# A four-layer graph network on one core: gathered rows as three bf16, and a layer's last blocks in one piece

## The chip, the core and the metric

The kernel runs on one core of a Trainium2 chip. The core has a matrix engine (TensorE, in the profile PE for matmuls and PEld for weight loads), VectorE (DVE), ScalarE (ACT) and GpSimd (POOL); SyncE (SP) issues most of the DMAs, and POOL issues the indirect ones, the gathers. The engines run on their own, each working through its own queue in order, and wait for each other by semaphores. The metric is the time of one execution on the device in microseconds.

## The reference

```python
N, E, C, NOUT, NL = 6250, 100000, 256, 64, 4

def agg(h):
    return jax.ops.segment_sum(h[src], dst, num_segments=N)

h = relu(layernorm(x0))          # 6250 x 256
x = h
for l in range(NL - 1):
    h = x + agg(x)
    h = relu(h @ W1s[l] + b1s[l])
    h = relu(h @ W2s[l] + b2s[l])
    x = h @ W3s[l] + b3s[l]
h = x + agg(x)
h = relu(h @ cW1 + cb1)
h = relu(h @ cW2 + cb2)          # 6250 x 64
out = x0 + (h @ cW3 + cb3)
```

All data are fp32. `src` and `dst` are drawn at random, and the edges come sorted by `dst`. So each of four layers sums, for every node, the rows of the nodes that point to it (16 on average), adds the node's own row, and sends the result through three matrices. In the kernel these are layers 0 to 3.

## The kernel before

The 6250 nodes are 49 blocks of 128 (the last has 106). `any_edges` is a fallback for inputs that are not as expected and does not run here; `sorted_edges` does the work. The next layer's first matrix is applied ahead: W3 of a layer is multiplied with W1 of the next once, early, so that each layer's table in DRAM (`tables[l]`, fp32, 256 columns) holds rows that have been through W1 already, and aggregation is done on those.

A layer aggregates its destination blocks in two ways, side by side.

- **Panels.** For 29 of the 49 blocks (25 in layer 0) the adjacency is kept as dense counts (uint8, built in layer 0, stored in DRAM as `mat`). A panel is 3 or 4 destination blocks. `product` runs over the 49 source blocks j of a panel, one *tick* each: four matmuls (L1334) of `XY[:, j]`, the rows of block j as an upper and a lower float32r part, against `a`, the counts cast from uint8 by ACT or DVE (`prepare`, three ticks ahead, AHEAD), into two PSUM tiles `agg`.
- **Gathered blocks.** The other 20 blocks (24 in layer 0) are done from lists of edges. Each block's edges stand in two halves of nine tiles of 128 edges. POOL issues one indirect DMA for each tile (L1198), which fetches 128 rows of the table into `rows`; DVE makes one-hot matrices `hot` (L1223); PE multiplies them (L1242) into `sums`. Each matmul has 32 stationary columns and uses one of four column strips of PE, chosen by half and quarter. A block is done in two *visits*, of three rounds each. In the trace a matmul of fp32 appears as two records.

Then `finish` adds the node's own row (`own`), transposes the result (L1264) and after the last block of a run calls `mlp`; `product` calls it for its panel. `mlp` spreads its work over the coming ticks: `second` (L1099, W2, with a relu on ACT), `third` (L1122, W3 times next W1, with the bias added on DVE into `z`, L1131) and `store`, which writes `z` to the next layer's table and, when all parts of the layer are kept, begins the next layer (`layers[l + 1].begin`).

**What sets the order.** The program order is written out by hand: each engine's queue is filled in the order of the calls. `tick` advances a clock `now` and runs what is `due`; `later(n, f)` puts f off by n ticks. A plan of the cost of each tick (`when`) spreads the visits of a layer evenly from LEAD = 75 units after `begin` to TAIL = 8 ticks before the layer's last tick. Gathers are issued up to three visits ahead. A gather of layer l + 1 reads rows from everywhere, so the first waits for the last store of layer l. As the last panel of a layer frees block j of `XY` (`used`), the next layer's rows are loaded back from the table (`back`, BACK = 3 at a time) or taken from `z` directly, and split into the upper part (ACT, L1055) and the lower (DVE, L1056).

**At a layer's end** the last gathered run is block 48 alone (`gone[-1]`), and the last panel is blocks 44 to 47 (40 to 43 in layer 0). Both go through `mlp` with `hurry`, their steps laid between the first ticks of the next layer's first panel.

Buffers that the change touches: `rows` 24 in layer 0 and 26 after it, `a` AHEAD + 4 after layer 0, `xt` 3 and `z` 2 in the last layer, `zz` 3.

Of the kernel before, what the change touches and what calls it, by code (L numbers as in the profile page):

```python
# [17 lines left out]
P = 128  # L18
# [378 lines left out]
def sorted_edges(  # L397
# [92 lines left out]
    eps = const.tile([P, 1], F32, name="eps")  # L490
    tables = [dram.tile([N, C], F32, name=f"table{l}") for l in range(NLAYER + 1)]
    w31d = [dram.tile([P, (KC + 1) * C], F32, name=f"w31_{l}") for l in range(NLAYER)]
    mats = [dram.tile([P, n, NT * P], U8, name=f"mat{p}") for p, (_, n) in enumerate(panels)]
# [407 lines left out]
    with tc.manual_schedule():  # L901
# [36 lines left out]
        def load_weights(l):  # L938
            w2 = load_w("w2", W2s[l] if l < NLAYER else cW2, work, nc.sync)
            if l < NLAYER:  # L940
                w3 = work.tile([P, KC + 1, C], F32, name="w3")
                nc.sync.dma_start(out=w3.rearrange("p k c -> p (k c)"), in_=w31d[l])
            else:
                w3 = late.tile([NOUT, C], F32, name="cw3", bufs=1)
                nc.sync.dma_start(out=w3, in_=cW3)
                row = late.tile([P, C], F32, name="cb3r", bufs=1)
                nc.sync.dma_start(out=row, in_=bass.AP(tensor=cb3.tensor, offset=cb3.offset,
                                                       ap=[[0, P], [1, C]]))
                w3 = (w3, row)
            weights[l] = w2, w3  # L950
# [88 lines left out]
        def later(n, fn):  # L1039
            due.append((now[0] + n, fn))  # L1040

        def tick():
            now[0] += 1
            run = [f for t, f in due if t <= now[0]]
            due[:] = [(t, f) for t, f in due if t > now[0]]
            for f in run:
                f()


# [3 lines left out]
        def split(j, m, z):  # L1053

            nc.scalar.copy(XY[:, j:j + m, :C], z[:, :m, :])  # L1055
            later(1, lambda: nc.vector.tensor_tensor(XY[:, j:j + m, C:], z[:, :m, :],  # L1056
                                                     XY[:, j:j + m, :C].bitcast(F32), OP.subtract))

        def reload(l, j):

            if (l, j) in used and (l, j) in kept and l < NLAYER:
                wanted.append((l, j))
                bring()
# [16 lines left out]
        def given():  # L1080
            lent[0] -= 1
            bring()

        def mlp(l, b0, n, h1, hurry):

# [18 lines left out]
            def third(i):  # L1104
                m = min(2, n - i)
                w3 = weights[l][1]
                if end:
                    xt = late.tile([P, 2, C], F32, name="xt", bufs=3)
                    if b0 + i + m == NT and LAST < P:
                        nc.vector.memset(xt[:, m - 1, :], 0.0)  # L1110
                    rows_io(x, b0 + i, m, xt, True)
                    nc.vector.tensor_tensor(xt[:, :m, :], xt[:, :m, :],
                                            w3[1][:, None, :].to_broadcast([P, m, C]), OP.add)
# [11 lines left out]
                if end:  # L1125
                    z = late.tile([P, 2, C], F32, name="z", bufs=2)
                    later(2, lambda: nc.vector.tensor_tensor(z[:, :m, :], v, xt[:, :m, :], OP.add))  # L1127
                    later(4, lambda: rows_io(out, b0 + i, m, z, False))
                    return
                z = work.tile([P, 2, C], F32, name="zz", bufs=3)  # L1130
                later(2, lambda: nc.vector.tensor_tensor(  # L1131
                    z[:, :m, :], v, w3[:, KC:, :].to_broadcast([P, m, C]), OP.add))

                def store():
                    rows_io(tables[l + 1], b0 + i, m, z, False)
                    blocks = range(b0 + i, b0 + i + m)
                    kept.update((l, j) for j in blocks)
                    if all((l, j) in used for j in blocks):
                        split(b0 + i, m, z)
                    else:  # L1140
                        for j in blocks:
                            reload(l, j)
                    if sum(1 for k, _ in kept if k == l) == NT:
                        layers[l + 1].begin(now[0])
                        later(1, lambda: load_weights(l + 1))

                later(3 - hurry, store)

# [9 lines left out]
        class Gathered:  # L1158
# [24 lines left out]
            def send(self, upto):  # L1183
                while self.sent < min(upto, self.n):
# [8 lines left out]
                    for k in self.tiles(rounds):  # L1193
                        for h in range(2):
                            t = gath.tile([P, C], F32, name="rows")
                            self.rows[g, h, k] = t
                            o = self.blocks[g][3] + h * TS + k
                            nc.gpsimd.indirect_dma_start(  # L1198
                                out=t, out_offset=None, in_=tables[self.l][:, :],
                                in_offset=bass.IndirectOffsetOnAxis(ap=idx[:, o:o + 1], axis=0),  # L1200
                            )
# [12 lines left out]
            def one_hots(self, v):  # L1214
# [3 lines left out]
                for r in rounds:  # L1218
                    hot = work.tile([P, 2, 2, Q], F32, name="hot", bufs=6)
                    for i, k in enumerate(ROUNDS[r]):  # L1220
# [8 lines left out]
            def add(self):  # L1229
# [8 lines left out]
                for r in rounds:  # L1238
                    for h in range(2):
                        for m, k in enumerate(ROUNDS[r]):  # L1240
                            if k is not None:
                                nc.tensor.matmul(  # L1242
                                    self.sums[(2 * h + m) * Q:(2 * h + m + 1) * Q, :C],
                                    self.hots[r, m][:, h, :], self.rows[g, h, k], start=(r == 0),
                                    stop=(r == (len(ROUNDS) - 2 if m == 0 else len(ROUNDS) - 1)))
                self.done += 1
# [5 lines left out]
            def finish(self, b, n, g, sums, own):  # L1252
                u = work.tile([P, C], F32, name="u", bufs=1)
                later(1, lambda: nc.vector.tensor_tensor(u, sums[:, :C], own[:, 0, :], OP.add))  # L1254
                if g == 0:
# [3 lines left out]
                def turn():  # L1259
# [11 lines left out]
                    if g == n - 1:  # L1271
                        mlp(self.l, b, n, h1, b == gone[-1][0])

# [9 lines left out]
        ahead = [2, 3]  # L1283
        LEAD, TAIL = 75, 8

# [30 lines left out]
        def product(l, p, ps_a, beside):  # L1316
# [25 lines left out]
            for c in range(KC):  # L1342
# [3 lines left out]
                else:  # L1346
                    nc.scalar.activation(h1[:, c, :w], agg[c][:, :w], AF.Relu,  # L1347
                                         bias=b1[l][:, c:c + 1])
            mlp(l, b0, n, h1, hurry)

# [13 lines left out]
        with tc.tile_pool(name="hots", bufs=1) as hots, tc.tile_pool(  # L1364
            name="ats", bufs=1
        ) as ats, tc.tile_pool(name="rings", bufs=AHEAD + 2) as rings, tc.tile_pool(
            name="gath", bufs=24
        ) as gath, tc.tile_pool(
# [17 lines left out]
        late = ctx.enter_context(tc.tile_pool(name="late", bufs=1))  # L1386
        rings = ctx.enter_context(tc.tile_pool(name="rings2", bufs=AHEAD + 4))
        gath = ctx.enter_context(tc.tile_pool(name="gath2", bufs=26))
        ps_a = ctx.enter_context(tc.tile_pool(name="ps_a2", bufs=4, space=PSUM))
# [68 lines left out]
```

## Time and profile before

| what | value |
|---|---|
| time, median of three runs | 2240.57 us (2235.93 to 2242.09) |
| the profiled execution's own time | 2230.63 us |
| its span, first to last instruction | 2228.8 us |
| granted TensorE clock, mean | 0.983 |
| gathers, L1198 | 1512, 982 ns each, 1484.3 us of POOL |
| panel matmuls, L1334 | 6076, 1454.7 us of PE |
| sums matmuls, L1242 | 3696 records, 281.5 us of PE |
| second and third matmuls, L1099 and L1122 | 164.3 and 140.0 us of PE |
| DMA | 395.56 MB, mean 177 GB/s |

A row of the table of groups gives the instruction's line, the engine, what it writes and reads, its count, then its busy time and its mean duration. Matmuls are pipelined, so the records overlap and a group's busy time is not the number of records times the mean. Where the text below speaks of the time of a group of matmuls, it is from the start of its first to the start of what follows on PE. The stages are: preparation and normalisation (0 to 188 us), layer 0 with the building of the counts (to 733), layers 1 (to 1231), 2 (to 1728) and 3 (to 2215), and the end. By windows, as busy us of the engine:

| window | PE | DVE | ACT | POOL | DMA share |
|---|---|---|---|---|---|
| 188 to 733 | 533.71 | 300.13 | 350.52 | 402.93 | 0.61 |
| 733 to 1231 | 490.72 | 164.42 | 160.52 | 347.89 | 0.58 |
| 1231 to 1728 | 491.31 | 162.47 | 159.26 | 349.09 | 0.57 |
| 1728 to 2215 | 471.75 | 166.80 | 142.56 | 350.60 | 0.59 |

### The profile page before, as it was taken

What the parts mean: (1) busy time and instruction counts of PE and PEld (TensorE: products, weight loads), DVE (VectorE), ACT (ScalarE), POOL (GpSimd) and SP (SyncE); (2) the same over time, 40 slices, a digit from 0 to 9 for tenths busy, and PEclk for the clock granted to TensorE, in tenths of its full rate; (3) what the DMA queues carried; (4) which work ended last, traced back from release to release, by engine and by line L of the source; (5) the groups of instructions that cost most, each with busy time, mean ns of one, the idle gap of its engine ahead of it and who ended that gap; (6) DMA issues with size and microseconds to landing.
All of it is one profiled execution on the core that took longest, in us unless ns stands there. A gap on an engine that the chain in (4) does not pass through costs nothing.

```text
span 2228.8 us, 35398 instructions
## 1 busy us (share of the span) xinstructions
PE 2118.0 (95%) x12356; PEld 1559.5 (70%) x12356; DVE 918.2 (41%) x2723; ACT 920.1 (41%) x1915; POOL 1521.5 (68%) x1570
## 2 busy tenths in 40 slices
PE   4778999999999999999999999999999999999998
PEld 2555766667776777778877777778877766677765
DVE  6667465445656522223323422223323423333332
ACT  3666565666667422223334322322324423222222
POOL 2337777777776477777774577777774577777773
PEclk9888999999999999999999999999999999999999
DMA  5436575565666655555655655555655655666663
GB/s 173 134 120 201 185 227 173 178 211 174 200 205 225 195 168 172 165 156 170 193 167 172 191 173 169 157 161 180 187 163 166 204 173 177 184 184 186 191 186 102
DMA packets 264100, 395.56 MB, mean 177 GB/s; under 512 B 36353, under 2 KB 210028, under 8 KB 263912
## 3 DMA queue, kind: packets, MB, share of 16 engines
q0 software_dynamic: 73920, 200.88, 30.2%
q1 hardware_dynamic: 187936, 189.68, 26.8%
q10 hardware_dynamic: 2056, 2.65, 0.4%
q8 instruction: 99, 1.62, 0.3%
q14 instruction: 89, 0.73, 0.1%
HBM read 335.81 MB, written 57.26 MB: 176 GB/s over the span
## 4 chain that ended last, share of the span: by engine, by line
PE 65%; DMA 4%; issue 2%; POOL 1%; ACT 0%; DVE 0%; SPq 0%; POOLq 0%; DVEq 0%
PE agg L1334 45%; PE sums L1242 8%; PE ps L1099 5%; PE ps L1122 4%; DMA rows<-table,idx 3%; POOL rows L1198 1%; PE ps L1119 1%; PE pt L1264 1%; PE bp L1010 1%; DMA xt<-in_x_dram 0%; ACT h L1347 0%; DMA own<-table 0%; DVE z L1127 0%; ACT at L1017 0%; ACT h L1268 0%
## 5 line engine op out<-in xcount | busy, mean ns | idle before, releaser
L1198 POOL DMA_INDIRECT rows<-table,idx x1512 | 1484.3, 982 | 614.0 <-issue 243.5
L1334 PE MATMUL agg<-a,XY 128*128 128x512 f32 (+1 forms) x6076 | 1454.7, 386 | 3.6 <-ACT a L1310 3.2
L1334 PEld LDWEIGHTS agg<-a,XY 128*128 128x128 f32 x6076 | 1085.4, 189 | 239.1 <-issue 81.0
L1310 ACT CAST a<-at 128x512 fp32r<-128x512 uint8 (+1 forms) x943 | 537.0, 579 | 650.3 <-PE agg L1334 585.2
L1312 DVE CAST a<-at 128x512 fp32r<-128x512 uint8 (+1 forms) x576 | 279.6, 490 | 498.7 <-PE agg L1334 455.0
L1242 PE MATMUL sums<-rows,hot 128*32 128x256 f32 x3696 | 281.5, 387 | 31.9 <-DMA rows<-table,idx 30.4
L1242 PEld LDWEIGHTS sums<-rows,hot 128*32 128x32 f32 x3696 | 119.4, 110 | 169.7 <-issue 54.7
L1017 ACT CAST at<-bp 128x392 uint8<-128x392 f32 x348 | 161.1, 490 | 142.8 <-PE bp L1010 139.9
L1099 PE MATMUL ps<-h,w 128*128 128x512 f32 (+5 forms) x392 | 164.3, 541 | 1.2 <-ACT h L1347 1.2
L1254 DVE TENSOR_TENSOR u<-sums,own 128x256 f32<-128x256 f32 x84 | 35.5, 423 | 291.7 <-PE sums L1242 291.7
L1010 PE MATMUL bp<-hi,lo 128*128 128x196 bf16 x928 | 136.0, 259 | 19.9 <-DVE hi L969 11.7
L1223 DVE TENSOR_TENSOR hot<-colf,rel 128x64 f32<-128x64 f32 x924 | 140.6, 217 | 12.3 <-PE sums L1242 11.9
L1122 PE MATMUL ps<-w,h 128*128 128x256 f32 x588 | 140.0, 379 | 0.0
L1010 PEld LDWEIGHTS <-lo 128*128 128x128 bf16 x928 | 71.9, 100 | 94.8 <-issue 43.9
L969 DVE TENSOR_TENSOR lo<-lanes,pairs 128x512 bf16<-128x512 bf16 x232 | 97.1, 419 | 84.0 <-PE bp L1010 58.4
L969 DVE TENSOR_TENSOR hi<-cols,pairs 128x784 bf16<-128x784 bf16 x232 | 129.6, 559 | 0.0
L1122 PEld LDWEIGHTS ps<-w,h 128*128 128x128 f32 x588 | 111.0, 189 | 15.7
L1268 ACT ACTIVATE h<-pt,bias 128x256 f32<-128x256 f32 (+1 forms) x92 | 36.9, 453 | 199.1 <-PE pt L1264 199.1
L1101 ACT ACTIVATE h<-ps,bias 128x512 f32<-128x512 f32 (+5 forms) x98 | 62.4, 637 | 109.6 <-PE ps L1099 109.6
L1131 DVE TENSOR_TENSOR zz<-ps,w 128x512 f32<-128x512 f32 (+1 forms) x81 | 51.7, 638 | 130.9 <-PE ps L1122 130.9
L1099 PEld LDWEIGHTS ps<-h,w 128*128 128x128 f32 (+1 forms) x392 | 68.2, 181 | 51.3 <-issue 29.4
L1019 DVE CAST at<-bp 128x392 uint8<-128x392 f32 x116 | 65.5, 565 | 91.9 <-PE bp L1010 90.3
(134 smaller groups left out, 716.6 us busy)
## 6 DMA issues: line engine op xcount, KB each, us to landing
at<-mat SPq DMA_DIRECT2D x133, 448.0 KB
at<-mat SPq DMA_DIRECT2D x84, 336.0 KB
rows<-table,idx POOLq DMA_INDIRECT x1512
mat<-at SPq DMA_DIRECT2D x29, 784.0 KB
table<-zz SPq DMA_DIRECT2D x66, 256.0 KB
back<-table SPq DMA_DIRECT2D x126, 128.0 KB
own<-table SPq DMA_DIRECT2D x80, 128.0 KB
xs<-in_x_dram SPq DMA_DIRECT2D x8, 768.0 KB
```

The lines of the kernel that those rows point to most:

```text
L969: nc.vector.tensor_tensor(o.rearrange("p q (n t) -> p q n t", t=2), values.rearrange("p (n t) -> p n t", t=2)[:, None, :, :].to_broadcast( ...
L1010: nc.tensor.matmul(bp[:, m * HW:(m + 1) * HW], lo[:, q + m, :], hi[:, q + m, :], start=True, stop=True)
L1017: nc.scalar.copy(o, v)
L1019: nc.vector.tensor_copy(o, v)
L1099: nc.tensor.matmul(ps[:mp, :w], weights[l][0][:, c, i * P:i * P + mp], h1[:, c, :w], start=(c == 0), stop=(c == KC - 1))
L1122: nc.tensor.matmul(o, h2[0][:, c, nodes], w3[:, c, :], start=(c == 0), stop=(c == KC - 1))
L1198: nc.gpsimd.indirect_dma_start(out=t, out_offset=None, in_=tables[self.l][:, :], in_offset=bass.IndirectOffsetOnAxis(ap=idx[:, o:o + 1], a ...
L1223: nc.vector.tensor_tensor(hot[:, i, :, :], colf[:, None, i * Q:(i + 1) * Q].to_broadcast([P, 2, Q]), rel[:, o + k:o + k + TS + 1:TS, None] ...
L1242: nc.tensor.matmul(self.sums[(2 * h + m) * Q:(2 * h + m + 1) * Q, :C], self.hots[r, m][:, h, :], self.rows[g, h, k], start=(r == 0), stop= ...
L1310: nc.scalar.copy(o, mat[l, p][j])
L1312: nc.vector.tensor_copy(o, mat[l, p][j])
L1334: nc.tensor.matmul(agg[c][:, :w], XY[:, j, o:o + P], a[:, :w], start=(j == 0 and half == 0), stop=(j == NT - 1 and half == 1))
```

## The change

Three things, in layers 1 to 3 and at the ends of layers 0 to 2.

1. Beside each table there is now `thirds[l - 1]`, the same rows as three bf16 parts whose sum is the fp32 value: 768 bf16, 1536 bytes a row in place of 1024. `store` puts each finished block on a list `waiting`; `in_thirds` makes the parts in four steps (ACT copies, DVE subtracts, ACT copies, DVE subtracts) and stores them; `one_step`, called once each tick, moves all jobs one step and starts a new one every three ticks. `tri` has two buffers, `left` one. Gathers of layers 1 to 3 read `thirds`, the one-hots are bf16, and each tile and strip has two bf16 matmuls: 512 columns (parts one and two side by side) and 256 columns (part three onto part one). `finish` adds both halves of `sums`.
2. The last run and the last panel of layers 0 to 2 no longer go through `mlp`. When both are there, `close` runs at one tick: four `second` steps, three `third` steps, the stores, then the thirds of all blocks that are left (`finish_thirds`), and only then `begin` of the next layer. Relus alternate between ACT and DVE.
3. TAIL goes from 8 to 5. Buffers: `rows` 22 and 23, `a` AHEAD + 3, `xt` 2; the last layer's `z` shares `zz`; the last layer's weights share the buffer of `w3`.

```diff
+    thirds = [dram.tile([N, 3 * C], BF16, name=f"thirds{l}") for l in range(1, NLAYER + 1)]
@@ tick
             for f in run:
                 f()
+            one_step()
@@
+        thirding, waiting = [], []
+
+        def in_thirds(l, j, z, of):
+            tri = work.tile([P, 1, 3 * C], BF16, name="tri", bufs=2)
+            t = [tri[:, 0, i * C:(i + 1) * C] for i in range(3)]
+            nc.scalar.copy(t[0], z)
+            yield
+            left = work.tile([P, C], F32, name="left", bufs=1)
+            nc.vector.tensor_tensor(left, z, t[0], OP.subtract)
+            yield
+            nc.scalar.copy(t[1], left)
+            yield
+            nc.vector.tensor_tensor(t[2], left, t[1], OP.subtract)
+            rows_io(thirds[l - 1], j, 1, tri, False)
+
+        def one_step():
+            for a in list(thirding):
+                a[1] += 1
+                if next(a[0], True):
+                    thirding.remove(a)
+            if waiting and (not thirding or thirding[-1][1] > 2):
+                a = waiting.pop(0)
+                job = in_thirds(*a)
+                next(job)
+                thirding.append([job, 1, a[3]])
+
+        def finish_thirds(upto):
+            while any(a[-1] <= upto for a in thirding + waiting):
+                one_step()
...
+        def rows_tile():
+            made[0] += 1
+            finish_thirds(made[0] - 3)
+            return work.tile([P, 2, C], F32, name="zz", bufs=3)
@@
+        def store(l, b, m, z, of):
+
+            blocks = range(b, b + m)
+            waiting.extend((l + 1, j, z[:, j - b, :], of) for j in blocks)
+            rows_io(tables[l + 1], b, m, z, False)
...
+        def close(l, run, panel):
...
+            def second(key, i):
...
+                ps = ps_m.tile([P, W], F32, name="ps")
+                for c in range(KC):
+                    nc.tensor.matmul(ps[:, :w], w2[:, c, i * P:(i + 1) * P], h1[:, c, :w],
+                                     start=(c == 0), stop=(c == KC - 1))
+                if i == 0:
+                    nc.scalar.activation(h2[b0][:, i, :w], ps[:, :w], AF.Relu,
+                                         bias=b2[l][:, i:i + 1])
+                else:
+                    nc.vector.tensor_scalar(h2[b0][:, i, :w], ps[:, :w], b2[l][:, i:i + 1], 0.0,
+                                            op0=OP.add, op1=OP.max)
...
+            for key in (run, panel):
+                for i in range(KC):
+                    second(key, i)
+            for key in (run, panel):
+                for i in range(0, key[1], 2):
+                    third(key, i)
+            finish_thirds(made[0])
+            free[0] = now[0] + 2
+            assert sum(1 for k, _ in kept if k == l) == NT
+            layers[l + 1].begin(now[0])
+            later(1, lambda: load_weights(l + 1))
@@ send
-                            t = gath.tile([P, C], F32, name="rows")
+                            if self.l:
+                                t = gath.tile([P, 3 * C], BF16, name="rows")
+                            else:
+                                t = gath.tile([P, C], F32, name="rows")
...
-                                out=t, out_offset=None, in_=tables[self.l][:, :],
+                                out=t, out_offset=None,
+                                in_=thirds[self.l - 1][:, :] if self.l else tables[0][:, :],
@@ add
+                            if self.l:
+
+                                nc.tensor.matmul(o, self.hots[r, m][:, h, :], t[:, :2 * C],
+                                                 start=(r == 0), stop=False)
+                                nc.tensor.matmul(o[:, :C], self.hots[r, m][:, h, :], t[:, 2 * C:],
+                                                 start=False, stop=stop)
@@ finish
+                def gather_up():
+                    nc.vector.tensor_tensor(u, sums[:, :C], own[:, 0, :], OP.add)
+                    if self.l:
+                        nc.vector.tensor_tensor(u, sums[:, C:], u, OP.add)
@@
-        LEAD, TAIL = 75, 8
+        LEAD, TAIL = 75, 5
@@
-        rings = ctx.enter_context(tc.tile_pool(name="rings2", bufs=AHEAD + 4))
-        gath = ctx.enter_context(tc.tile_pool(name="gath2", bufs=26))
+        rings = ctx.enter_context(tc.tile_pool(name="rings2", bufs=AHEAD + 3))
+        gath = ctx.enter_context(tc.tile_pool(name="gath2", bufs=23))
```

`close`'s `third` does what `mlp`'s does, with the bias added at once and `store` called directly.

## The prediction

> **What bounds the kernel now.** I read the page's busy shares first, then the boundary between layers 1 and 2 in the timelines of POOL, SP and PE, then who PE waited for. Page, part 1:
>
> ```profile
> PE 2118.0 (95%) x12356; PEld 1559.5 (70%) x12356; DVE 918.2 (41%) x2723; ACT 920.1 (41%) x1915; POOL 1521.5 (68%) x1570
> ```
>
> PE looks like the only bound. POOL's timeline says otherwise (start, duration, then the idle time before it):
>
> ```profile
> 1202.48 1.03 POOL L1198 DMA_INDIRECT rows<-table,idx  x1 [0.30 <-issue]
> 1244.45 0.95 POOL L1198 DMA_INDIRECT rows<-table,idx  x1 [40.94 <-DMA own<-table]
> 1245.70 0.95 POOL L1198 DMA_INDIRECT rows<-table,idx  x1 [0.31 <-PE agg L1334]
> ...
> 1702.01 0.95 POOL L1198 DMA_INDIRECT rows<-table,idx  x1 [0.30 <-PE agg L1334]
> 1741.56 0.95 POOL L1198 DMA_INDIRECT rows<-table,idx  x1 [38.60 <-DMA own<-table]
> ```
>
> A gather is 0.95 busy and 0.30 between: one per 1.26 us. Layer 2's 360 gathers run from 1244.45 to 1702.01, 457.6 us or 1.27 each, so POOL never pauses; then it stands still until layer 3's table is complete. So a layer is a ring: some 457 us of gathers, then a turn of about 40 us from the last gather to the next layer's first (PE and SP timelines):
>
> ```profile
> 1227.48 2.22 PE L1334 MATMUL agg<-a,XY 128*128 128x512 f32 x8
> 1230.00 1.98 PE L1099 MATMUL ps<-h,w 128*128 128x512 f32 x4 [0.30 <-ACT h L1347]
> ...
> 1241.38 0.37 SPq L501 DMA_DIRECT2D table<-zz  x1
> ...
> 1257.16 0.62 PE L1242 MATMUL sums<-rows,hot 128*32 128x256 f32 x2 [0.95 <-DMA rows<-table,idx]
> ```
>
> I call E the end of a layer's last panel, read so at each boundary: E1 731.2, E2 1229.7 (1227.48 + 2.22), E3 1726.6, E4 2215.0. The last table store is issued at E2 + 11.7, the first gather is at E2 + 14.7 (3.1 after the store), the first visit's last tile is met at 1257.2, 3.9 after its gather started at 1253.25. E1 to E2 is 498.5, E2 to E3 496.9, E3 to the end 502.2. PE's waits, layer 2 and then layer 3 (total, times, longest):
>
> ```profile
> PE sums L1242 <- DMA rows<-table,idx: 3.8, 4, 1.4
> ```
> ```profile
> PE sums L1242 <- DMA rows<-table,idx: 14.2, 14, 3.5
> ```
>
> In layer 2 PE is the bound, with some 12 us of slack on POOL at the end (last gather 1702.0, last visit 1714.6); in layer 3, where PE has less to do, POOL is. **Both count, nearly equal**, and whatever moves the first gather moves a layer's end.
>
> **The change, part by part.**
>
> *The sums on PE.* One visit now:
>
> ```profile
> 1109.24 1.50 PE L1242 MATMUL sums<-rows,hot 128*32 128x256 f32 x24
> 1110.67 9.64 PE L1334 MATMUL agg<-a,XY 128*128 128x512 f32 x40
> ```
>
> 24 matmuls in 1.43 us (start to next start). A full-width fp32 matmul of 256 columns (ps of L1122, x8 in 1.54) takes 0.19 to 0.22, so 24 in turn would be about 5 us: the four 32-column strips run side by side, six groups of 0.216 plus 0.13. fp32 needs 2 clocks per column; bf16 one, as bp's 196 columns show (L1010, bf16: four are through in 0.30 to 0.36, timeline at 601). A bf16 pair of 512 and 256 columns is 0.216 + 0.109 = 0.325 per round, three rounds 0.98, a visit 1.11: **0.32 saved, 40 visits, 12.8 us of PE per layer**. A rule speaks against it: the Trainium skill ("TensorE: Matmul & The Clock Gate", Part 3, what overlaps and what doesn't) has matmuls start and end in strict program order. A strip's two passes are neighbours in the program, so by the rule each pair would hold up the next strip: 4 x 0.216 per round, 2.6 us a visit, before and after alike. The row has 1.43 with the same neighbours, so the strips don't hold each other up, and I take 1.11.
>
> *Gathers of 1536 B rows.* Issue: rows of 512 B (L741, 72 rows) take 0.95, 1024 B (L680, 98 rows) 0.97, ours 0.95; no dependence on bytes, so I take 0. Upper end: L649's 5632 B rows took 1.55; linear, 0.118 ns a byte, gives +0.06. Transfer: gathers hold 30.2% of the DMA engines by queue; half as much again and the new 192 KB stores bring layers 1 to 3 from 0.57 (table by windows) to about 0.8. Landing 3.9 becomes, I estimate, 4.6 (ends 3.9 and 8).
>
> *Making the thirds.* Per block two ACT copies (L1055's 128x256 cast: 0.407), two DVE subtractions (L1056: 0.419), one store: 49 x 0.8 = 41 us on ACT and DVE per layer, one block in three ticks. At 0.33 busy each in layers 1 to 3 (same table) this hides behind PE, and so does the second add into u. In layer 0 ACT is 0.64 and DVE 0.55 busy, and PE waits there already for ACT (3.5) and DVE (1.9): +3 us (ends 1 and 8). DVE traffic seems to lengthen gathers: layer 0 with its busy DVE averages 1.32 per gather against 1.27. A quarter more DVE work: +2 us per layer on POOL (0 to 5). TAIL 5 drops three ticks of PE between last visit and E.
>
> *Fewer buffers* (rows 26 to 23, `a` 7 to 6, xt 3 to 2): 0. POOL's idle before a gather is 0.30 throughout, so it waits for no buffer; casts run three ticks ahead and six buffers hold that; at the end the last xt loads are queued on SP behind the run's output store already. If POOL did wait for rows, each wait would go straight into the ring.
>
> *The boundary.* Now the path that sets the end. PE, from E: run's second 0.8, panel's second 2 x 1.35, run's third 0.7, a wait for DVE's eviction (0.75) of about 0.4, panel's third 2 x 1.54: last third starts at E + 6.5, all done by 8.0. Before, a third that started at 1238.74 had its store issued at 1241.38, 2.64 later; so z is there at E + 9.1, and ACT's XY copy of it (0.62), queued ahead of the thirds, ends at 9.8. Only then do five blocks (48, 44 to 47) go through copy, subtract, copy, subtract: 1.66 + three hand-overs of 0.07 = 1.87. There are two `tri` buffers, so block 3 waits for the store of block 1, and block 5 for that of block 3. A load's landing, issue to a waiting ACT, is 1.95 to 2.1 at best in this trace; I take 2.3 for a store. One generation is 1.87 + 0.15 + 2.3 = 4.3: second at 14.1, third at 18.4, its last store at 20.4. POOL starts 3.1 later, at 23.5; with a second DMA for block 48's ten rows, **24, against 14.7**. Queued behind this on ACT and DVE are the casts `a` of the new panel: only three ticks are prepared, so PE stands from E + 10 to about E + 22; SP holds own, back and weight loads behind the stores, all wanted later than that.
>
> The first visit is reached after 15 ticks and needs 8 tiles: 24 + 8.8 + 4.6 = E + 37.4. PE has 19.2 us of work in that time (7.3 + 60 matmuls 10.8 + 1.1): **18 us idle at each of three boundaries**. The granted clock: 0.97 over 1250 to 1300, after stalls under 2 us, so 1.7 us lost. The skill's rule (same page, Part 1) has the clock halve after about 3.4 us idle; by the row one boundary in three would pay, by the rule each, 1.7. The gaps are long: I take the rule, half hidden in waits for rows.
>
> *Sum per layer, E to E.* PE: 496.9 - 5.6 of waits (rows 3.8, `a` 0.9, others) - 12.8 + 18.2 + about 0.9 = 497.6. POOL: 24 + 457.6 + 2 + 4.6 + 0.3 + 5.8 (24 matmuls after the last visit) = 494.3. I take 497: layer 1 -1.5, layer 2 +0.1. Layer 3 is POOL's: 24 + 458.9 + 2 + 4.6 + 0.3 + 5.8 + 14.7 (after E4: 13.8 now, run's third later) = 510.3 against 502.2: +8.1. Layer 0: +3. Total +9.7 on the profiled 2230.6 (span 2228.8). The median of the runs, 2240.57, is 10 us above that execution; the same difference gives **2250**.
>
> **Rivals.**
> *A, faster: 2225.* The turn stays nearly as short as before: the thirds of the last blocks overlap the close's matmuls, or stores land in a microsecond, and gathers start at E + 16. Then POOL gives 494.3 - 8 = 486.3, PE with 8 us less idle 489: layer 1 -9.5, layer 2 -7.9, layer 3 +0.1, layer 0 +2: -15. For it: 12.8 us of PE a layer are really gone. Against: ACT's in-order queue puts the copies behind the last z, and the two buffers put three landings in a row. It decides below about E + 20.
> *B, gather issue grows with bytes: 2315.* +0.06 x 1080 gathers = 65. Against: 512 and 1024 B rows cost the same.
> *C, DMA crowding: 2270.* Landing 8 us, not 4.6, and slower stores in the chain: 7 us per boundary. For it: 0.8 busy on average, fetches of `at` in bursts.
> *D, strips take turns: 2400.* 120 visits of 2.6, some +50 per layer.
>
> **Chances.** Sum 0.50 (its own range 2240 to 2260), A 0.27, C 0.13, B 0.07, D 0.03. A measurement can't tell less than 0.3%, 6.7 us, from no change. Above 2247: 0.33 of the sum's half, B, C, D: 0.56. Within: 0.17 of the sum and 0.02 of A, 0.19. Below: 0.25. Range 2217 to 2283: B, D and the far side of A are left out.
>
> **What would show it.** In the profile after: sums about 1.1 a visit; POOL still 1.26 a gather; the first gather 22 to 26 after the panel's end, following tri stores in three generations; PE idle about 18 at each boundary, first for `a`, then for rows; E to E near 497. A first gather before E + 20, or gathers of over 1.3, would overturn it.

## The result and the profile after

The changed kernel takes **2302.99 us** (median of four runs, 2301.2 to 2304.1) against 2241.33 for the kernel before in the same session: a ratio of **1.0279, 95% interval 1.0262 to 1.0297**. The direction was forecast, 2250 was not: it lies 53 us too low, and the time is outside the range. The profiled execution has a span of 2300.9 us, 72.1 more than before.

The page, part 1, of the kernel after:

```profile
PE 2112.3 (92%) x12356; PEld 1568.8 (68%) x12356; DVE 1054.1 (46%) x3083; ACT 1016.3 (44%) x2203; POOL 1542.8 (67%) x1570
```

PE is busy 5.7 us less, although each of 120 visits now needs 1.10 us and not 1.43. ACT and DVE have grown by 96 and 136 us and are still idle more than half the time. By shares, nothing here is worse. The layers have to be read one by one, E to E:

| | layer 0 (E1) | layer 1 | layer 2 | layer 3 to the end | first gather after E1, E2, E3 |
|---|---|---|---|---|---|
| before | 731.2 | 498.5 | 496.9 | 502.2 | 15.0, 14.7, 15.0 |
| forecast | +3 | 497 | 497 | 510.3 | 24 |
| after | 770.4 | 510.9 | 507.1 | 512.6 | 25.0, 22.6, 22.8 |

The profiled execution of before (2230.63 us) is one of its fastest, so a difference of two or three microseconds in a layer means little against it; where that matters, the ratios decide.

The end of a layer came as forecast, and so did layer 3. Layer 0 is 39 us longer and not 3, layers 1 and 2 are 14 and 10 us past the forecast. Layers 0 to 2 have something in common that layer 3 lacks: thirds are made while they run. First the boundary, as shown of before (timelines of POOL, PE and SP of the kernel after):

```profile
1260.77 0.95 POOL L1302 DMA_INDIRECT rows<-thirds,idx  x1 [0.30 <-issue]
1303.89 0.95 POOL L1302 DMA_INDIRECT rows<-thirds,idx  x1 [42.18 <-DMA own<-table]
1305.15 0.95 POOL L1302 DMA_INDIRECT rows<-thirds,idx  x1 [0.30 <-issue]
```
```profile
1281.13 4.77 PE L1162 MATMUL ps<-h,w 128*128 128x128 f32 x16
1285.73 4.73 PE L1177 MATMUL ps<-w,h 128*128 128x256 f32 x20
1290.11 2.44 PE L1457 MATMUL agg<-a,XY 128*128 128x384 f32 x12
1301.69 10.71 PE L1457 MATMUL agg<-a,XY 128*128 128x384 f32 x48 [9.14 <-DVE a L1435]
```
```profile
1293.54 0.73 SPq L508 DMA_DIRECT2D thirds<-tri  x2
1294.96 6.56 SPq L503 DMA_DIRECT2D thirds<-tri  x4
1301.57 0.91 SPq L503 DMA_DIRECT2D own<-table  x2
```

E2 is 1281.3. PE does three ticks (12 matmuls) and stands for 9.1 us, for `a`; the stores of the thirds run from E + 12.3 to E + 20.2; the first gather is at E + 22.6. A gather is still 0.95 with 0.30 between: 1536 B rows cost no more to issue.

Now layer 0. The view of waits over 188 to 770 us, kernel after (who waits, for what, then the total in us, how often, the longest), and the same view of ACT and PE in layer 1:

```profile
ACT tri L1068 <- DMA thirds<-tri: 33.8, 14, 6.6
DVE left L1071 <- ACT tri L1068: 23.7, 12, 5.6
PE bp L1012 <- DVE hi L971: 11.0, 11, 4.1
PE bp L1012 <- ACT at L1019: 9.4, 14, 2.2
PE agg L1457 <- ACT a L1433: 8.3, 2, 4.4
```
```profile
ACT tri L1068 <- DMA thirds<-tri: 50.7, 26, 5.2
PE agg L1457 <- ACT a L1433: 18.2, 8, 12.3
```

(The longest wait in layer 1, 12.3, is the boundary's.) ACT, less than half busy, stands 33.8 us in layer 0 for a DMA that is on no path of the computation: the store of an earlier block's thirds. One such wait, from the timelines of ACT, DVE, SP and PE merged:

```profile
582.03 0.41 ACT L1068 CAST tri<-zz 128x256 bf16<-128x256 f32 x1
584.58 0.41 ACT L1068 CAST tri<-zz 128x256 bf16<-128x256 f32 x1
585.39 0.42 DVE L1075 TENSOR_TENSOR tri<-left,tri 128x256 bf16<-128x256 f32 x1
588.77 0.53 SPq L1035 DMA_DIRECT2D at<-mat  x1
589.40 1.41 SPq L503 DMA_DIRECT2D thirds<-tri  x2
593.22 0.41 ACT L1068 CAST tri<-zz 128x256 bf16<-128x256 f32 x1 [6.44 <-DMA thirds<-tri]
594.10 1.65 PE L1457 MATMUL agg<-a,XY 128*128 128x384 f32 x4 [3.97 <-ACT a L1433]
```

The block whose copy starts at 582.03 has its thirds complete at 585.81 (585.39 + 0.42). Its store is issued at 589.40, behind a fetch of `at` in SP's queue, and its packets end at about 592.7. The next copy but one (584.58 has the other buffer) needs its buffer; it stands at the head of ACT's queue from 586.78 on and starts at 593.22. The casts of `a` are queued behind it, and PE is without work for 3.97 us. A block's copy comes two ticks after the block's before it, not three: the new block begins at the step at which the count of the last reaches 3, and that count is 1 when it starts. So with two buffers a copy stands in ACT's queue **one tick** behind the store that it needs.

How long the stores take, worked out from the trace's DMA packets (1536 B on SP's queue, 128 for a block): of the 42 stores issued in layer 0 the last packet ends 2.7 us after the issue (median), 4.1 in one case of ten, 5.3 at the longest; from the end of the last subtraction 2.8, 5.3 and 7.1. Over all three tables one in ten ends within 1.5 us. In 24 cases in layer 0 the copy follows so closely that the store may still be under way; it comes to the head of ACT's queue 0.9 to 5.8 us after the issue, twice even before it. 14 of the 24 wait, and start 0.4 to 1.1 us after the store's last packet. Within these waits and the 1.5 us after each, PE is idle for some 23 us.

The wait shown is one of the three longest. In it, and in one of 6.6 us at 665, SP's queue had held the store back for 3.6 and 3.5 us, behind a fetch of `at`: these two make 13.1 of the 33.8 us. In the third (5.0 us at 548) the store was issued at once.

### The profile page after: what moved, and what is told of

It is laid out like the page before. It is cut to its first block, busy times and chain, and to the rows that moved or that the text cites. A ratio compares the mean times of both kernels' runs of the same rounds, so it can differ in the third digit from the quotient of the medians.

```text
span 2300.9 us, 36354 instructions
## 1 busy us (share of the span) xinstructions
PE 2112.3 (92%) x12356; PEld 1568.8 (68%) x12356; DVE 1054.1 (46%) x3083; ACT 1016.3 (44%) x2203; POOL 1542.8 (67%) x1570
## 4 chain that ended last, share of the span: by engine, by line
PE 76%; DMA 11%; DVE 5%; ACT 4%; issue 2%; POOL 1%; SPq 0%; ACTq 0%; DVEq 0%; POOLq 0%
PE agg L1457 49%; PE ps L1213 6%; PE ps L1236 5%; DMA thirds<-tri 4%; DMA rows<-thirds,idx 4%; PE sums L1353 4%; PE bp L1012 3%; PE sums L1358 3%; PE sums L1355 2%; PE bp L868 1%; POOL rows L1302 1%; DMA rows<-table,idx 1%; PE ps L1233 1%; PE pt L1384 1%; ACT at L1019 1%
## 5 line engine op out<-in xcount | busy, mean ns | idle before, releaser
L1457 PE MATMUL agg<-a,XY 128*128 128x512 f32 (+1 forms) x6076 | 1477.9, 391 | 53.2 <-ACT a L1433 34.5
L1302 POOL DMA_INDIRECT rows<-thirds,idx x1080 | 1056.1, 978 | 462.1 <-issue 154.2
L1457 PEld LDWEIGHTS agg<-a,XY 128*128 128x128 f32 x6076 | 1104.7, 193 | 283.3 <-issue 72.9
L1302 POOL DMA_INDIRECT rows<-table,idx x432 | 449.5, 1041 | 199.9 <-issue 71.3
L1353 PE MATMUL sums<-rows,hot 128*32 128x512 bf16 x1320 | 139.9, 385 | 28.7 <-DMA rows<-thirds,idx 27.1
L1213 PE MATMUL ps<-h,w 128*128 128x512 f32 (+4 forms) x344 | 151.1, 562 | 0.9 <-ACT h L1470 0.9
L1328 DVE TENSOR_TENSOR hot<-colf,rel 128x64 bf16<-128x64 f32 (+1 forms) x924 | 140.5, 220 | 11.7 <-PE sums L1358 11.2
L1068 ACT CAST tri<-zz 128x256 bf16<-128x256 f32 x147 | 59.9, 408 | 178.6 <-DMA thirds<-tri 136.6
L1071 DVE TENSOR_TENSOR left<-zz,tri 128x256 f32<-128x256 f32 x147 | 62.6, 426 | 115.3 <-ACT tri L1068 108.5
L1355 PE MATMUL sums<-rows,hot 128*32 128x256 bf16 x1320 | 113.9, 274 | 0.0
L1236 PEld LDWEIGHTS ps<-w,h 128*128 128x128 f32 x528 | 99.7, 189 | 14.4
```

Source lines behind the costliest of these rows:

```text
L1213: nc.tensor.matmul(ps[:mp, :w], weights[l][0][:, c, i * P:i * P + mp], h1[:, c, :w], start=(c == 0), stop=(c == KC - 1))
L1236: nc.tensor.matmul(o, h2[0][:, c, nodes], w3[:, c, :], start=(c == 0), stop=(c == KC - 1))
L1302: nc.gpsimd.indirect_dma_start(out=t, out_offset=None, in_=thirds[self.l - 1][:, :] if self.l else tables[0][:, :], in_offset=bass.Indirec ...
L1328: nc.vector.tensor_tensor(hot[:, i, :, :], colf[:, None, i * Q:(i + 1) * Q].to_broadcast([P, 2, Q]), rel[:, o + k:o + k + TS + 1:TS, None] ...
L1353: nc.tensor.matmul(o, self.hots[r, m][:, h, :], t[:, :2 * C], start=(r == 0), stop=False)
L1355: nc.tensor.matmul(o[:, :C], self.hots[r, m][:, h, :], t[:, 2 * C:], start=False, stop=stop)
```

## The experiments

Each ratio is against the kernel before, run on the same chip in the same session. E1 and the layers are of the profiled execution, as in the table above.

| | ratio (95% interval) | E1 | layer 1 | layer 2 | layer 3 to the end |
|---|---|---|---|---|---|
| e1 thirds begun less often | 1.0146 (1.0116 to 1.0176) | 751.9 | 503.5 | 500.8 | 509.4 |
| e9 three `tri` | 1.0103 (1.0088 to 1.0119) | 745.5 | 503.9 | 501.2 | 508.7 |
| e2 four `tri` | 1.0046 (1.0028 to 1.0063) | 738.4 | 500.7 | 497.1 | 506.5 |
| e3 layer 1 in fp32 | 1.0087 (1.0056 to 1.0117) | 732.7 | 505.1 | 509.9 | 509.0 |
| e4 one-piece end alone | 0.9994 (0.9984 to 1.0003) | 732.4 | 500.8 | 502.0 | 502.1 |
| e6 thirds alone | 1.0262 (1.0245 to 1.0280) | 765.1 | 511.5 | 509.1 | 507.6 |
| e5 stores from ACT's queue | 1.0415 (1.0380 to 1.0449) | 765.7 | 529.5 | 527.7 | 510.3 |
| e10 thirds' work, not stored | 1.0035 (1.0022 to 1.0049) | 738.1 | 501.9 | 501.6 | 500.4 |
| e7 four `tri`, fp32 gathers | 1.0057 (1.0040 to 1.0073) | 741.0 | 501.9 | 501.3 | 502.4 |
| e8 thirds early at the end | 1.0039 (1.0025 to 1.0053) | 742.4 | 499.2 | 495.4 | 506.8 |
| e11 one-piece end, old buffers | 0.9995 (0.9986 to 1.0003) | 730.3 | 499.7 | 500.5 | 503.1 |
| e12 early, reordered | **0.9973** (0.9961 to 0.9986) | 741.4 | 492.7 | 491.0 | 506.6 |

**Does the wait for the buffer make the time?** e1 lets fewer blocks be under way, e2 and e9 add buffers.

```diff
-        def one_step():                                           # e1
+        def one_step(between=5):
...
-            if waiting and (not thirding or thirding[-1][1] > 2):
+            if waiting and (not thirding or thirding[-1][1] > between):
...
-                one_step()
+                one_step(2)
-            tri = work.tile([P, 1, 3 * C], BF16, name="tri", bufs=2)  # e2 (rows 19 and 21)
+            tri = work.tile([P, 1, 3 * C], BF16, name="tri", bufs=4)
```

> A block's thirds are begun six ticks after the block before, not three (only while a layer runs; at its end they follow each other as in the changed kernel). Same work, same bytes, same buffers, but a tri buffer is taken again 12 ticks after its last use and not 6. Theory (ACT and DVE, in order, stand behind a tri buffer whose store has not landed, and PE waits for the casts behind it): the waits of ACT for the thirds' store in layer 0 and inside layers 1 and 2 go, layer 0 ends near 737 us and not 770, layers 1 and 2 lose some 8 us each; about 2250 us. Rival 'work' (the added copies and subtractions overload ACT and DVE in layer 0): no change, 2303. Rival 'crowding' (1536 B rows and the stores slow every transfer): no change, 2298 to 2303.

> Four tri buffers instead of two, paid for with three row tiles less in layer 0 (19) and two less after it (21). Theory (the wait for a store two blocks back): as with the slower pace, layer 0 ends near 737, and at the end of a layer only the fifth block waits for a landing, so the first gather goes from 25 us after the layer's last panel to about 17: some 2225 us. Rivals 'work' and 'crowding': 2300, a little more if the row tiles are short. Rival 'buffers' (fewer row tiles hold POOL back): slower than 2303.

> Three tri buffers, 20 and 22 row tiles. The traces so far show a new block every two ticks while a layer runs, so with two buffers a copy comes one tick after the store that it needs, with four five ticks, and here three. The stores' last packets end 2.5 us (median) and up to 5.3 us after the issue, and a tick is 0.9 to 1.7 us. Theory (what counts is the distance in ticks between a store and the copy that needs its buffer): most copies find their buffer free, a few wait 1 to 3 us; layer 0 ends between the 752 us of the slower pace (also three ticks) and 738 of four buffers, 2250 to 2265 us. Rival (two blocks at once were the trouble, and any spare buffer cures it): as with four, 2243 to 2248; rival (fewer row tiles took part in the gain or loss): not between.

e1 gave 2268.26 us and not 2250. Its text has the pace wrong: a job leaves the list after three steps, so a block follows every three ticks (12 panel matmuls between the copies in the trace), for two in the changed kernel. That puts the copy three ticks after the store, and 22.3 us of ACT's waits are left of 33.8 in layer 0. e2 puts it five ticks after (2246.57 us) and e9 three (2260.83, as expected); in e9 8.5 us are left, in two waits. e2's own forecast was missed by 21 us: layer 0 ends where it should, but the first gather comes at E + 20.6 to 21.1 and not at 17, and the time is not 2225. In e2's view of waits over 188 to 738 us ACT has none, and of PE's rows (1.9 and 3.5 us before the change) this is left:

```profile
PE bp L1012 <- DVE hi L971: 4.6, 13, 1.0
PE bp L1012 <- ACT at L1019: 3.3, 9, 0.7
```

So the length follows the distance in ticks between a store and the copy that needs its buffer: one tick 2.79% over before, three 1.03 and 1.46%, five 0.46%. Ticks are not all of it: of e1's 22.3 us, 14.4 are two waits for stores that SP's queue had held for 4.4 and 3.5 us, and at the boundaries e1 still has two buffers (first gathers as in the changed kernel). Two buffers in place of four cost 2.33%, 52 us of the 62; some 2 to 4 us at each boundary are in it, where e2's first gather comes sooner. "Work" and "crowding" would have left e1, e2 and e9 at the changed kernel's time, and so would a lack of row tiles, of which e2 has the fewest.

**Where do the thirds cost, and what does the one-piece end cost?** e3 gathers layer 1 from `tables[1]` in fp32, so layer 0 makes no thirds. e4 has the end in one piece and no thirds at all. e6 has the thirds, but the old end.

```diff
-            waiting.extend((l + 1, j, z[:, j - b, :], of) for j in blocks)   # e3
+            if l:
+                waiting.extend((l + 1, j, z[:, j - b, :], of) for j in blocks)
...
-            waiting.extend((l + 1, j, z[:, j - b, :], of) for j in blocks)   # e4
...
-            if l == NLAYER:                                           # e6, TAIL 8
-                mlp(l, *what, True)
-                return
+            mlp(l, *what, True)
+            return
```

> Layer 1 gathers its rows in fp32 from the table as before the change, so layer 0 makes no thirds; layers 2 and 3 are as in the changed kernel, and the last panel and run still go in one piece at all three ends. Every theory that blames the thirds: layer 0 ends at 731 to 735 us, and the first gather of layer 1 starts some 13 us after it; about 2258 us. Rival 'fewer buffers' (22 row tiles for 24 in layer 0) or another part of the change: layer 0 still ends near 770, 2295 us.

> The one-piece end of a layer alone: all rows fp32, no thirds made, TAIL 5, the changed kernel's buffers. The one piece has the last z about 3 us sooner than the old order, and nothing behind it, so the first gather should start 12 us after the last panel's end and not 14.7: -1.5 to -3 us per boundary, about 2233 to 2239 us, if the end of a layer is bound by that chain. If the one piece (PE idle while its evictions run, fewer ticks after the last visit) costs time itself: 2245 to 2255.

> Thirds alone: the end of a layer goes tick by tick as before the change (TAIL 8), and the next layer's gathers begin when the last third is stored; two tri buffers. Theory: layer 0 loses the same (ends near 770), and the first gather comes 25 to 28 us after the last panel's end, for 25 and 22.7 with the one-piece end; 2303 to 2313 us, so the one piece gives a few us back at most. If the one-piece end itself costs time beside the thirds: below 2298.

e3: E1 is 732.7, so layer 0's 39 us are the thirds made in it, and nothing else of the change; layer 2 stays at 509.9. e4: the first gather comes at E + 13.0 to 13.4 (12 expected, 15 before), and yet the ratio is 1 within its interval, and layers 1 and 2 are no shorter than before: an earlier gather brought nothing where PE has as much to do as before. e6: 2293.54 us, below the 2298 that was to show a cost of the one piece; but before was 7 us faster in that session too, and by ratio e6 (1.0262) and the whole change (1.0279) have overlapping intervals. Its first gathers come at E + 21.0 to 21.8, and not at 25 to 28: with thirds made, the old end has them 1.5 to 3.2 us sooner than the one piece (22.6 to 25.0). So the few us back that were expected of the one piece with thirds did not show, nor did a cost that these runs could tell; without thirds it is worth nothing.

**Is a store slow because of SP's queue, or because of the traffic?**

```diff
             nc.vector.tensor_tensor(t[2], left, t[1], OP.subtract)
-            rows_io(thirds[l - 1], j, 1, tri, False)
+            yield
+            rows_io(thirds[l - 1], j, 1, tri, False, nc.scalar)
...
```

> The thirds' stores are issued by ACT on its own queue, one tick after the last subtraction, instead of by SP; still two tri buffers. Theory 'order': the store lands late because it stands in SP's queue behind fetches of at (448 KB) and stores of mat (784 KB) issued before it; on a queue of its own it lands in some 2 to 3 us, ACT's waits for it in layer 0 fall from 33.8 us to under 10, layer 0 ends at 740 to 748, about 2255 to 2265 us (ACT spends some 0.5 us more on each issue). Rival 'bandwidth' (the 16 engines are full, whichever queue asks): the waits stay near 30 us, 2295 to 2305.

2331.14 us, slower than either said. Layer 0, of which both spoke, is 5 us shorter than in the changed kernel (765.7 for 770.4); layers 1 and 2 are 19 and 21 us longer, and that makes the time. The edit cures what it was made for: SP's queue held a store back by over 1 us in 4 cases of 42 in the changed kernel's layer 0, and the two waits of over 6 us behind them are now 2.5 and 2.7 us. But it makes the other stores late, since they are issued a tick on and stand behind ACT's other work: over 1 us between subtraction and issue in 22 of 42 cases. From the end of the subtraction to the last packet it is now 4.0 us (median) for 2.8, and ACT's waits are 38.0 us in layer 0 and 78.6 in layer 1, for 33.8 and 50.7. From the issue on, a store on ACT's own queue takes 2.3 us (median), 5.0 in one case of ten and 6.9 at the longest, much as on SP's. So another queue is no cure, but the run does not rule out the order in SP's queue as a part of the cause, and does not measure the traffic's share.

**What is the work worth, and what do the bf16 rows bring?** e10 makes the thirds and does not store them (the stores and the reading of thirds are left out; the sums are those of before). e7 is e2 with the sums from the fp32 table.

```diff
-            rows_io(thirds[l - 1], j, 1, tri, False)                  # e10
...
-                                in_=thirds[self.l - 1][:, :] if self.l else tables[0][:, :],
+                                in_=tables[self.l][:, :],             # e7 and e10, one fp32 pass
```

> The copies and subtractions of the thirds are made as in the changed kernel (two tri buffers), but not stored, and the sums take the fp32 rows; the one-piece end stays. What is left out is the stores and the reading of thirds. It measures ACT's and DVE's added work alone, against the one-piece end alone (0.9994 of before). Theory (the prediction's term: +3 us in layer 0, ends 1 and 8, else hidden): 1.000 to 1.004 of before, layer 0 ends at 733 to 741. Rival 'work' (ACT and DVE in layer 0 are overloaded): layer 0 ends past 755, 1.012 or more.

> As with four tri buffers, and the thirds are made, stored and waited for, but the sums take the fp32 rows of the table as before the change (their computation is the old one, nothing reads the thirds). It measures what the bf16 rows give. Theory (0.32 us of PE saved per visit, gathers of 1536 B no dearer): 40 visits lose 12.8 us of PE per layer, of which part is hidden in waits: 2262 to 2280 us, visits of 1.43 us. Rival 'crowding' (the wide rows and their DMA traffic cost as much as the sums save): 2240 to 2250.

e10: 0.41% over e4, some 9 us, 5.7 of them in layer 0 (738.1 against 732.4): the work costs what the prediction's term allowed (1 to 8). And e2, which makes and stores the thirds, has E1 at 738.4: with four buffers the stores add nothing to layer 0. e7 is a miss: 2247.18 against e2's 2246.57, no difference. The windows say why (start and end, length, busy PE, PEld, DVE, ACT and POOL with counts, granted clock, DMA share, GB/s); layer 2 of e7, then of e2:

```profile
1243.00:1744.00 501.00, 490.41 (x2795) 375.08 (x2795) 201.45 (x607) 190.87 (x408) 350.92 (x360) 0.99 0.64 191
```
```profile
1239.00:1736.00 497.00, 481.96 (x2797) 374.17 (x2796) 209.76 (x627) 191.12 (x408) 350.61 (x360) 0.98 0.78 240
```

bf16 rows take 8.5 us of PE away (12.8 forecast), at a lower clock; but e7's gathers do not wait for the thirds' stores, though its text says so, and begin at E + 13 in place of E + 20.7. So the run does not measure bf16 alone. In layer 2 bf16 is 4 us ahead, in layer 3, where POOL is the bound, 4 us behind.

**A version that is faster than before, by little.** With the waits gone, layers 1 and 2 of e2 were taken to be POOL's: first gather at E + 20.7, 460 us of gathers, and 17 to 20 us from the last gather to the next E. e8 puts each z through its thirds before the XY copies; e11 gives e4 its old buffers back, and TAIL 8 in layer 3; e12, with four `tri` buffers as e8, evicts the three z ahead of the thirds, delays the XY copies by two ticks, casts three `a` more ahead, and has TAIL 3 (8 in layer 3) and LEAD 100.

```diff
+                if key is run:                                        # e12
+                    prepare(now[0] + AHEAD + 2, True)
...
+                ends_.append((b0 + i, m, z))
+                if len(ends_) > 1:
+                    finish_thirds(made[0] - 1)
...
+            for k, (b, m, z) in enumerate(ends_):
+                later(2 + k, lambda b=b, m=m, z=z: (split(b, m, z) if ...
-        LEAD, TAIL = 75, 5
+        LEAD, TAIL = 100, [3, 3, 3, 8]
```

> Four tri buffers, and in the one-piece end each z goes into its thirds as soon as it is evicted, ahead of the copies into XY, which come last; the casts of three more a tiles are put ahead of it all. Theory (the chain from the last z to the last third sets the first gather): first gather 15 to 17 us after the last panel's end instead of 20.6, and PE stands 2 to 3 us less for a: 2226 to 2234 us. Rival (PE, not the gathers, sets a layer's length once the waits are gone, so an earlier gather is worth nothing): 2243 to 2247.

> The one-piece end alone (fp32 rows, no thirds), with the buffers of before (rows 24 and 26, one a tile more) and TAIL 5 for layers 0 to 2 but 8 for layer 3, where nothing follows that a short end would bring forward. If the smaller buffers and TAIL 5 in layer 3 ate the gain of the earlier gathers: 2222 to 2230, 0.993 to 0.997. If the layers' length is PE's work and not the gathers' start: 0.998 to 1.001.

> Four tri buffers and bf16 rows; at a layer's end the three z are evicted before their turn in the thirds, XY copies come two ticks later, three a casts by ACT while the panel's first matmuls run, first visit due after 20 ticks (LEAD 100), TAIL 3 (8 in layer 3). Theory (layers 1 and 2 are POOL's: first gather + 457 us + the end after the last gather): first gather at 15 to 17 us, 2 us less after the last gather: layers 1 and 2 at 489 to 493, layer 3 at 502; 2220 to 2230 us, 0.993 to 0.998. Rival (PE's lower clock and waits have become the bound): 495 or more per layer, 2238 to 2245.

e8 missed: the third z's eviction stood in DVE's queue behind the second z's subtractions (at E + 12.3), and the first gather came only 1.7 us sooner. 2243.46 us lies where its rival put it, but with so small a step the rival was not tested. e11: nothing again; e4's smaller buffers had cost no time, and the end alone brings nothing. e12: **2230.78 us**, 0.27% under before (0.14 to 0.39) and 3% under the changed kernel. The first gather is at E + 18.0 to 19.9, not at 15 to 17; layers 1 and 2 are 492.7 and 491.0, layer 3 is 506.6 and not 502. Its PE shows what the bf16 sums are worth when nothing stands in the way (windows, layer 2 of e12):

```profile
1234.00:1725.00 491.00, 479.02 (x2798) 370.65 (x2797) 206.75 (x625) 192.10 (x410) 352.82 (x360) 1.00 0.79 243
```

479.0 us of PE against 491.3 in the same layer before, at the same clock: 12.3 less, where 12.8 was forecast. Several edits went in together, and how much each gave was not tried.

## Why the prediction was wrong

**The step that failed** is "Making thirds": "49 x 0.8 = 41 us on ACT and DVE per layer, one block in three ticks. [...] this hides behind PE", with +3 us for layer 0. It costed the copies and subtractions, and those were right (5.7 us in layer 0 by e10). It did not cost what a copy waits for. The two buffers and the landing were counted at the boundary, block by block, and nowhere else. Inside a layer a panel hands over three or four blocks within two ticks, the third and fourth need the buffers of the first and second one tick after their stores, and from the last subtraction to its last packet a store takes 1.5 to 7.1 us. The prediction (and the description of the change) read the pace as three ticks; it is two. Even three would not have been enough, as e1 and e9 show. Priced: two buffers for four, +2.33%, 52 us. Without that term (e2) the profiled execution's span is 2242.7, where the prediction's sum gives 2238.5, and e2's layers are 738.4, 500.7, 497.1 and 506.5 for a forecast of 734, 497, 497 and 510.3: the sum fits better than its parts, which miss by up to 4 us both ways. How the 52 us divide between traffic, which slows a store, and SP's queue, which delays a few, stays open.

**Granted clock.** The prediction took 0.9 us a boundary from the rule in the Trainium skill ("TensorE: Matmul & The Clock Gate", Part 1: cold after about 3.4 us of idling) and nothing inside a layer. The three stalls of 4.0 to 4.4 us in layer 0 fit the rule, each with half clock behind it. After the one of 3.97 us at 590 the windows of the kernel after read

```profile
594.10:599.20 5.10, 5.10 (x19) 4.14 (x19) 2.99 (x7) 4.36 (x12) 3.88 (x5) 0.50 0.62 177
600.00:606.00 6.00, 6.00 (x56) 4.52 (x56) 4.13 (x13) 3.81 (x10) 3.27 (x3) 1.00 0.59 181
```

half clock for 5.1 us, then full. But half clock also followed a stall of 2.2 us, which is shorter than the rule's 3.4:

```profile
396.34 0.33 PE L1012 MATMUL bp<-hi,lo 128*128 128x196 bf16 x2 [2.20 <-ACT at L1019]
```
```profile
397.90:401.30 3.40, 3.40 (x12) 2.49 (x11) 2.76 (x7) 2.82 (x8) 2.48 (x4) 0.50 0.52 143
```

So the rule's length is no safe margin here; what decides below it, these runs do not show. Stalls that were not forecast carry this with them: in layer 0 PE is busy 545.1 us against 534.5 in e2 for the same matmuls. Of the 32 us between the two kernels' E1, 10.6 are slower matmuls and the other 21.4 idle time. At the boundaries PE is idle 12.9 us each (18 forecast) and busy 25.1 where 19.2 us of work were counted: together they are what was forecast, with the clock (0.82 over these stretches) a larger part. That the sum fits while both terms are 5 to 6 us off is in part luck.

**The sums** were right. 24 records take 1.10 us from start to next start (1.11 forecast, 1.43 before); in layer 1 of the kernel after:

```profile
903.07 0.41 PE L1353 MATMUL sums<-rows,hot 128*32 128x512 bf16 x4
903.30 0.29 PE L1355 MATMUL sums<-rows,hot 128*32 128x256 bf16 x4
...
904.17 0.50 PE L1457 MATMUL agg<-a,XY 128*128 128x512 f32 x1
```

The column rates used in the sum stand in the records as a ratio: 0.216 us for a group of 256 fp32 columns, and 0.216 again for one of 512 in bf16 (in this visit's second round). How many clocks that is, no trace here tells. The rule of strict program order would have had 2.6 us before and after. In `kernel.py` a strip's second pass stands right behind its first, yet the four strips start the first pass together and then the second. Nor is that order fixed. In the first visit of layer 2 one strip was ahead of the other three by its times, and began its next round before their second passes:

```profile
1313.16 0.27 PE L1355 MATMUL sums<-rows,hot 128*32 128x256 bf16 x1
1313.27 0.38 PE L1353 MATMUL sums<-rows,hot 128*32 128x512 bf16 x1
1313.29 0.29 PE L1355 MATMUL sums<-rows,hot 128*32 128x256 bf16 x3
```

The measurement decides: the strips run side by side, each at its own pace. Rival D falls.

**The gathers** were right: 0.95 and 0.30 as before, for 1536 B; rival B falls. In layers 1 and 2 the 360 gathers took 465 and 463 us, not 459.6; e2 and e12 have 460 and 461, so the rest was POOL waiting for row tiles that a stalled PE freed late (up to 2.8 us at once behind the sums in layer 1, for 0.4 in e2). **DMA** share rose to 0.76 (0.8 forecast). Crowding, rival C, was looked for in the gathers' landing: the first visit of layer 2 meets its last tile at 1317.91, 5.2 after that tile's gather started at 1312.71 (4.6 forecast, 3.9 before). It was found in the stores instead, where it decides because a copy waits for them: the seven stores right after E1, with the DMA share at 0.38 (779 to 795), end 1.5 to 1.8 us after their issue, the 42 before it 2.7 us in the median at 0.62.

**Fewer buffers**: 0 was right for the time (e11 against e4). Its reason was not: in layer 1 of e4, where the gathers start sooner, POOL waits up to 4.1 us at once behind the sums that free its row tiles (0.3 before), and no layer's end shows it as PE sets the length there. **The boundary**: 24 forecast, 25.0, 22.6 and 22.8 measured, with two of ACT's waits for landings (1.20 and 1.00 us). Rival A, gathers at E + 16, was reached by no kernel here that makes thirds: even e12 has E + 18.0.

**Layer 3**: 510.3 forecast, 512.6 measured, and no thirds are made there. It was the one layer without the missing term. Here too the parts offset each other: the last gather starts 3 us sooner than forecast, from there to E4 it is 2 us more, and the end after E4 takes 18.1 us and not 14.7.

## What to carry to other kernels

When work is added to an engine that is half idle, count for each instruction what it waits for, not only how long it takes: an in-order engine hands every wait at its head to all that is queued behind, as ACT's 6.4 us did to the casts of `a`, and through them to PE. A buffer that is emptied by a store comes free when the store has landed (here 0.4 to 1.1 us after its last packet the waiting copy began), so the number of buffers has to cover the landing time, under this kernel's own traffic, divided by the time between two blocks of the *burst* that fills them, not by the average over a layer. And a shorter chain at one end of a stage is worth nothing while another engine sets the stage's length: the one-piece end brought 0 with fp32 sums. e12, with the bf16 sums, four buffers and gathers that start sooner than e2's, is the one kernel under before, and which of its edits did that is not shown.

## What the runs showed of the hardware

A 192 KB store into DRAM ended its last packet 1.5 to 6.8 us after its issue on SP's queue in the changed kernel, with the DMA share at 0.62 to 0.76 over layers 0 to 2, and up to 6.9 us on ACT's. TensorE's granted clock fell to half after a stall of 2.2 us as well as after those of 4. Bf16 matmuls in 32-column strips kept the strips' overlap: 24 passes (four strips, three rounds, two passes each) in 1.10 us. And 2.3% of the kernel hung on waits of an engine that was 44% busy; the one row that named them was ACT's wait for `thirds<-tri`.
